# One VectorE product for two states at a time in a selective scan that runs beside attention

## The chip, the cores and the metric

One Trainium2 chip, one core of it. The metric is the device time of one execution in microseconds (us). The kernel before took a median of 3411.59 us in 3 runs (3409.64 to 3413.27).

## The reference, cut to what matters

The input is a batch of 4 images, 128 channels of 64 x 64. Four layers follow one another: attention over the 4096 positions with a residual (layer 0), two quantized 3 x 3 convolutions (layer 1), a Mamba block with a group norm (layer 2), and attention again (layer 3). The change is in layer 2. Its core is a scan over the 4096 positions of an image, for 256 inner channels and 16 states each:

```python
def step(h, inp):
    dt_t, B_t, C_t, x_t = inp
    dA = jnp.exp(dt_t[..., None] * A)
    dBx = dt_t[..., None] * B_t[:, None, :] * x_t[..., None]
    h = dA * h + dBx
    y = jnp.einsum('bdn,bn->bd', h, C_t)
    return (h, y)
...
return jnp.swapaxes(ys, 0, 1) + xc * D
```

`B_t` and `C_t` are the same for all channels and differ by state; `A` differs by channel and state.

## The kernel before, in words

**Tiling.** The 256 inner channels lie as 128 partitions x 2 halves (index h). The 4096 positions of an image are cut into 8 blocks of 512 (TB). A *group* g is one block of one image: 4 images x 8 blocks are 32 groups, and each has 16 states n. One *state* m = 16 g + n is the unit of the scan: 512 of them. Tiles that hold both halves of one block are 128 x 2 x 512 fp32, 1024 elements in a partition.

**What one state does.** Nine instructions, the load among them:

- fetch (SP's queue, L1086): row n of B and row n of C, repeated over all 128 partitions, into a `bc` tile (3 buffers); it may start when the product with C of three states earlier is done;
- decays (ScalarE, L1099, one for each half): `da = exp(A dt)` into PSUM, one buffer for each half, so it waits for the scan that read the last one;
- the **B product** (VectorE, L1126): `hs = ud * B`, with `ud = dt x`, 1024 elements, for both halves in one instruction; `hs` has 3 buffers, so it waits for the addition of three states earlier;
- the **scans** (VectorE, L1134, one for each half, 512 elements): `hs[t] = da[t] hs[t-1] + hs[t]` in place, which begins from `hlast`, the last column of the block before;
- the last column (ScalarE, L1109): copied from `hs` to `hlast` before `hs` is overwritten, except in an image's last block;
- the **C product** (VectorE, L1116): `hs = hs * C` in place, which waits for that copy;
- the **addition** (GpSimd, L1151): `y = y + hs`, which waits for the C product.

After the 16th state of a group GpSimd also does the **gate** (L1155), `y = y * sz`. VectorE's order is B product of state m, C product of state m - 1, the two scans of state m.

**Preparation of a group** (L884 to L996). TensorE, ScalarE and VectorE make `xc`, `sz`, `dt`, `ud` and the start of `y` from layer 1's output. The softplus for `dt` uses a tile `sp` (Abs at L971, Exp at L976, read last by VectorE at L982), followed by L984, L986 and L990 on VectorE.

**Everything else runs beside it.** While layer 2 works on one image, TensorE and ScalarE do an attention stage of another. The eight attention stages follow each other in the order layer 0 of images 0, 1 and 2, layer 3 of 0, layer 0 of 3, layer 3 of 1, 2 and 3. The last has no scan beside it. An attention stage makes blocks of energies (L535), their exponentials (ScalarE, L553) and the products with the values (L615, L624, L643). Layer 0's operands are split into a high and a low part by way of a tile `h` (L443 and L445). The convolutions' instructions on VectorE are L804, L816, L833, L838 and L840; those at the end of an attention block are L694, L705, L735 and L765; L1020 and L1062 belong to the group norm.

**What sets the order.** All instructions are written by chains (generators: `scans`, `additions`, `fetches`, `preparation`, `convolutions`, `energies` and so on). Before each instruction a chain yields an `op`: engine, planned time, the marks that it needs, and flags. The class `Order` keeps a clock for every engine and always takes the chain whose next instruction has the lowest key, planned start + 0.15 x the chain's rank on that engine (`RANKS`). The outcome is a fixed order of each engine's queue; on the chip an instruction waits only for the data and buffers that it needs. One flag matters here: `port=True` for VectorE instructions, and always for GpSimd, books a planner's clock that both share, so that the plan never lays two such instructions over each other. On the chip nothing enforces this part of the plan.

Of the kernel before, what the change touches and what calls it, by code (L numbers as in the profile page):

```python
# [8 lines left out]
F32 = mybir.dt.float32  # L9
# [11 lines left out]
P = 128  # L21
# [10 lines left out]
DS = 16  # L32
# [17 lines left out]


RANKS = {
    "layer1_weights": dict(SP=-5.3, ACT=9.6, DVE=17.6, PE=-7.5),
    "layer2_weights": dict(SP=11.2, ACT=5.6, DVE=13.0),
    "parts": dict(ACT=0.8),
    "first": dict(ACT=-1.6, DVE=-2.8, PE=-4.9),
    "convolutions": dict(ACT=2.0, DVE=4.4, PE=4.2),
    "preparation": dict(SP=16.0, PE=2.4, ACT=0.9, DVE=3.0),
    "output": dict(PE=3.0, ACT=0.0, DVE=1.7, SP=-3.8),
    "lasts": dict(ACT=-0.0),  # L60
    "energies": dict(PE=3.5),
    "exponentials": dict(ACT=1.4),
    "products": dict(PE=5.1),
    "decays": dict(ACT=0.8),
    "scans": dict(DVE=4.7),
    "additions": dict(POOL=9.6),
    "fetches": dict(SP=-17.0),
    "accumulations": dict(DVE=15.7),
    "totals": dict(PE=-1.0),
    "images": dict(SP=9.9),  # L70
    "high_low": dict(ACT=4.8, DVE=2.3),
    "copy": dict(ACT=2.5),
    "finish0": dict(DVE=2.9, ACT=-1.9, PE=-5.1),
    "stage_input": dict(SP=9.0),
    "residual": dict(SP=2.8),
    "finish3": dict(PE=4.1, DVE=3.8, ACT=3.2, SP=-14.6),
}


class Order:  # L80
# [7 lines left out]
    def __init__(self):  # L88
        self.clock = dict(PE=7.0, ACT=5.0, DVE=6.0, POOL=6.0, SP=7.0)
        self.marks = {}  # L90
        self.chains = []
        self.table = self.tiles = None
        self.bank = 0.0
        self.port = 0.0
        self.end = (0.0, None)

# [9 lines left out]
    def mark(self, *key):  # L106
        self.marks[key] = self.end
# [1 line left out]
    def known(self, time, *key):  # L109
        self.marks[key] = time, None  # L110

    def release(self):
        self.bank = self.end[0]

    def run(self):
        while self.chains:
            best = None
            for item in self.chains:
                engine, time, needs, bank, table, port, lag, tiles, who = item[3]
                if any(k not in self.marks for k in needs) or (bank and self.bank is None):  # L120
                    continue
                start = self.clock[engine]
                for t, e in [item[2], *(self.marks[k] for k in needs)]:
                    start = max(start, t + (self.HOP if e != engine else 0.0))
                if bank:
                    start = max(start, self.bank + self.HOP)
# [12 lines left out]
            item[2] = self.clock[engine], engine  # L139
            self.end = self.clock[engine] + lag, engine  # L140
            if bank:
                self.bank = None
# [35 lines left out]
def conv_seq_kernel(ctx: ExitStack, tc: tile.TileContext, i: dict, out: bass.AP):  # L178
# [107 lines left out]
    def layer1_weights(k):  # L286
        unit, dt = ((LEVELS, F32R), (LEVELS * LEVELS, FP8))[k - 1]
        yield op("SP", 0.3, lag=4.0)
        w = mam.tile([P, 2, TB], F32, tag="hs", name=f"w{k}", bufs=3)
# [127 lines left out]
    def operands(s):  # L417
# [19 lines left out]
        def high_low(o, g, key, bias, low, n):  # L437

            c = len(lows)
            lows.append(("low", s, c))  # L440
            yield op("ACT", 0.2 + n * 1e-3, (*key, "in"), *lows[c - 1 : c])
            h = att.tile([P, 2 * TB], F32R, tag="h", name="h", bufs=1)
            nc.scalar.activation(h[:, 0:n], g, AF.Identity, bias=low[1], scale=low[0])  # L443
            yield op("DVE", 0.06 + n * 1.2e-3)
            nc.vector.scalar_tensor_tensor(o, g, bias, h[:, 0:n], ALU.add, ALU.subtract)  # L445
            mark(*key)
            mark(*lows[c])

# [113 lines left out]
    def accumulations():  # L562
        for t in filter(added, range(len(stages) * NS)):
            k, q = divmod(t, NQ)
            for h in range(2):
# [4 lines left out]
                    need.append(("total", k - 1))  # L570
                yield op("DVE", 1.25, *need, port=True)
                if q == 0:
                    accs[k] = att.tile([P, 2, 2, CB], F32, tag="acc", name="acc", bufs=1)
                other = ps[t, 0] if q == 0 else accs[k]
                nc.vector.tensor_add(accs[k], ps[t, h], other)  # L575
            mark("acc", t)
# [307 lines left out]
    def preparation():  # L884
        for g in range(NG + 1):
# [70 lines left out]
            for h in range(2):  # L956
                yield op("PE", 0.98, *need, bank=True, who=who)
                if h == 0:
                    dt, ud, y = (pair(t, t, 2) for t in ("dt", "ud", "y"))
                    a = pair("sp", "sp", 1)  # L960
                ps = gtile("dt_ps")
                for k in range(2):
                    nc.tensor.matmul(
# [3 lines left out]
                        start=True,  # L967
                        stop=True,
                    )
                yield op("ACT", 0.69, who=who)  # L970
                nc.scalar.activation(a[:, h, :], ps, AF.Abs, bias=bdt[:, h : h + 1])  # L971
                yield op("ACT", 0.68, who=who)
                nc.scalar.activation(dt[:, h, :], ps, AF.Relu, bias=bdt[:, h : h + 1])
                release()
            yield op("ACT", 1.06, table="exp", who=who)
            nc.scalar.activation(a, a, AF.Exp, scale=-1.0)  # L976
# [3 lines left out]
            nc.scalar.activation(ud, y, AF.Ln)  # L980
            yield op("DVE", 1.22, port=True, who=who)
            nc.vector.scalar_tensor_tensor(y, y, 1.0, a, ALU.subtract, ALU.subtract)  # L982
            yield op("DVE", 1.22, port=True, who=who)
            nc.vector.tensor_sub(ud, ud, y)  # L984
            yield op("DVE", 1.22, port=True, who=who)
# [92 lines left out]
                mark("x2", b, k)  # L1078

    def fetches():  # L1080
        for m in range(NM):
            g, n = divmod(m, DS)
            need = [("c", m - 3)] if m > 2 else []
            yield op("SP", 0.1, ("bc_d", g), *need, lag=5.0)
            bcs[m] = bc = mam.tile([P, 2, TB], F32, tag="bc", name="bc", bufs=3)
            nc.sync.dma_start(  # L1086
                out=bc, in_=live["bc", g][:, n, :].unsqueeze(0).to_broadcast([P, 2, TB])
            )
            if n == DS - 1:
                live.pop(("bc", g))  # L1090
            mark("bc", m)

    def decays(h):
        for m in range(NM):
# [7 lines left out]
            mark("da", m, h)  # L1102

    def lasts():
        for m in range(NM):
            g, n = divmod(m, DS)
            if g % NTB < NTB - 1:
                yield op("ACT", 0.2, ("s", m, 1))
                nc.scalar.copy(hlast[:, n, :], hss[m][:, :, TB - 1])  # L1109
                mark("last", m)  # L1110
            else:
                order.known(0.0, "last", m)

    def readout(m):
        hs = hss[m]
        nc.vector.tensor_mul(hs, hs, bcs.pop(m)[:, 1:2, :].to_broadcast([P, 2, TB]))  # L1116
        mark("c", m)

    def scans():
        for m in range(NM):  # L1120
            g, n = divmod(m, DS)
            need = [("add", m - 3)] if m > 2 else []
            yield op("DVE", 1.2, ("bc", m), ("ud", g), *need, port=True)
            ud = live["in", g][1]
            hss[m] = hs = pair("hs", "hs", 3)
            nc.vector.tensor_mul(hs, ud, bcs[m][:, 0:1, :].to_broadcast([P, 2, TB]))  # L1126
            if n == 0:
                mark("begun", g)
            if m:
                yield op("DVE", 1.13, ("last", m - 1), port=True)  # L1130
                readout(m - 1)
            for h in range(2):
                yield op("DVE", 1.19, ("da", m, h))
                nc.vector.tensor_tensor_scan(  # L1134
                    hs[:, h, :],
                    das.pop((m, h)),
                    hs[:, h, :],
                    hlast[:, n, h : h + 1] if g % NTB else 0.0,
                    ALU.mult,
                    ALU.add,  # L1140
                )
                mark("s", m, h)
        yield op("DVE", 1.13, ("last", NM - 1), port=True)
        readout(NM - 1)

    def additions():
        for m in range(NM):
            g, n = divmod(m, DS)
            yield op("POOL", 2.36, ("c", m), ("y", g))
            y = live["in", g][2]  # L1150
            nc.gpsimd.tensor_tensor(y, y, hss.pop(m), ALU.add)  # L1151
            mark("add", m)
            if n == DS - 1:
                yield op("POOL", 2.4, ("sz", g))
# [534 lines left out]
```

## Time and profile before

| what | value |
|---|---|
| median of the runs | 3411.59 us |
| the profiled execution, its own time | 3404.14 us |
| its span (first to last instruction) | 3402.3 us |
| busy TensorE, VectorE, ScalarE, GpSimd | 3123.7, 3024.0, 2573.9, 1319.4 us |
| mean granted TensorE clock | 0.979 |
| additions L1151 / gates L1155 on GpSimd | 512 of 2376 ns / 32 of 3127 ns |
| decays L1099 on ScalarE | 1024 of 690 ns |
| fetches L1086, 512 KB each, issue to landing | 512, median 4.8 us (3.4 to 9.0) |
| first and last scan | 173 us and 3076 us |

How it is read: in a line of instruction groups come the line and engine, the operation, output and inputs with shape and type, the count, then busy time and mean ns of one, then the engine's idle time just before these instructions and what ended most of it. In a list of waits come the waiting engine, tile and line, what ended the wait, the total us, how many times, and the longest. In a timeline come start and length in us, engine, line, operation, the tiles, the count, and in brackets the idle time before it. VectorE's instructions overlap in it by some 0.08 us, so costs are read from start to start. GpSimd's lengths include any time in which an issued instruction stood still.

### The profile page before, as it was taken

How to read it: one execution, taken by the hardware profiler on the slowest of the kernel's cores; microseconds unless marked ns; L12 is line 12 of the kernel's file. 1: busy time of each engine (PE TensorE's matmuls, PEld its weight loads, DVE VectorE, ACT ScalarE, POOL GpSimd, SP SyncE). 2: the span in 40 equal slices, each digit the busy share in tenths (PEclk: the TensorE clock that was granted, in tenths of full speed). 3: DMA queues.
4: the chain of work that ended last, by engine and by line, in shares of the span. 5: the costliest groups of instructions: out<-in, count | busy, mean ns of one | idle time of the engine just before them, and what ended most of it. 6: DMA issues, size and time to landing. Idle time of an engine off the chain costs nothing.

```text
span 3402.3 us, 69611 instructions
## 1 busy us (share of the span) xinstructions
PE 3123.7 (92%) x29359; PEld 2249.8 (66%) x29359; DVE 3024.0 (89%) x2828; ACT 2573.9 (76%) x3899; POOL 1319.4 (39%) x565
## 2 busy tenths in 40 slices
PE   7999989999889999998988999999899899998998
PEld 5887768788678776555547888755455455555665
DVE  3199999999999999999999999999999999994554
ACT  4588877878788786878777888877788787865554
POOL 0044444444334444444434444444444445441000
PEclk9999999999999999999999999999999999999999
DMA  3033343333443334444443333444444444330000
GB/s 80 23 97 101 89 121 97 98 101 98 111 111 101 97 94 125 105 110 109 111 138 97 97 91 93 120 97 110 124 111 108 130 104 116 105 111 18 8 11 12
DMA packets 194179, 321.72 MB, mean 95 GB/s; under 512 B 44352, under 2 KB 46784, under 8 KB 193856
## 3 DMA queue, kind: packets, MB, share of 16 engines
q1 hardware_dynamic: 193568, 316.32, 35.1%
q8 instruction: 232, 3.80, 0.4%
q10 hardware_dynamic: 288, 0.85, 0.1%
q14 instruction: 91, 0.75, 0.1%
HBM read 300.35 MB, written 16.78 MB: 93 GB/s over the span
## 4 chain that ended last, share of the span: by engine, by line
DVE 50%; PE 29%; issue 10%; ACT 9%; DMA 2%; SPq 0%; DVEq 0%; ACTq 0%
DVE hs L1134 21%; DVE hs L1126 12%; DVE hs L1116 9%; PE e L535 8%; PE us L624 6%; PE us L615 6%; ACT p L553 2%; ACT da L1099 2%; PE us L643 1%; DMA bc<-bc_d 1%; DVE ud L984 1%; PE proj L458 1%; PE proj L500 1%; PE conv L777 1%; ACT L1099 1%
## 5 line engine op out<-in xcount | busy, mean ns | idle before, releaser
L1151 POOL TENSOR_TENSOR y<-y,hs 128x1024 f32<-128x1024 f32 x512 | 1216.7, 2376 | 1751.3 <-DVE hs L1116 1699.0
L553 ACT ACTIVATE p<-e 128x1024 f32<-128x1024 f32 x1024 | 1011.3, 1017 | 186.1 <-PE e L535 86.5
L1134 DVE TENSOR_TENSOR_SCAN hs<-da,hlast,hs 128x512 f32<-128x512 f32 x896 | 1098.8, 1263 | 8.2 <-ACT da L1099 8.1
L615 PE MATMUL us<-v,p 128*128 128x129 f32 x8192 | 1028.7, 281 | 16.4 <-ACT us L671 16.4
L615 PEld LDWEIGHTS us<-v,p 128*128 128x128 f32 x8192 | 959.6, 193 | 79.1 <-ACT us L671 22.7
L1099 ACT ACTIVATE da<-dt,late 128x512 f32<-128x512 f32 x1024 | 701.5, 690 | 249.8 <-DVE hs L1134 247.0
L1116 DVE TENSOR_TENSOR hs<-hs,bc 128x1024 f32<-128x1024 f32 x512 | 674.0, 1316 | 20.7 <-ACT hlast L1109 20.5
L1126 DVE TENSOR_TENSOR hs<-ud,bc 128x1024 f32<-128x1024 f32 x512 | 661.0, 1291 | 0.4
L535 PE MATMUL e<-it,v 64*128 64x256 f32 x4096 | 543.6, 401 | 64.3 <-ACT p L553 63.1
L624 PE MATMUL us<-p,v 128*32 128x256 f32 x8192 | 512.7, 386 | 22.0 <-ACT ss L680 22.0
L535 PEld LDWEIGHTS e<-it,v 64*128 64x128 f32 x4096 | 374.9, 190 | 222.6 <-ACT p L553 115.5
L624 PEld LDWEIGHTS us<-p,v 128*32 128x32 f32 x8192 | 244.8, 110 | 243.6 <-issue 70.3
L535 PE MATMUL e<-it,j 64*128 64x256 f32 x2048 | 222.4, 319 | 42.4 <-ACT p L553 39.2
L535 PEld LDWEIGHTS e<-it,j 64*128 64x128 f32 x2048 | 146.1, 187 | 127.3 <-ACT p L553 67.4
L643 PE MATMUL us<-p,ones 128*32 128x256 f32 x3072 | 204.3, 383 | 0.0
L575 DVE TENSOR_TENSOR acc<-p,acc 128x1024 f32<-128x1024 f32 x96 | 117.4, 1223 | 60.4 <-ACT p L553 56.1
L1109 ACT COPY hlast<-hs 128x2 f32<-128x2 f32 x448 | 84.8, 189 | 102.3 <-DVE hs L1134 93.5
L1134 DVE TENSOR_TENSOR_SCAN hs<-da,hs 128x512 f32<-128x512 f32 x128 | 149.4, 1203 | 0.9 <-ACT da L1099 0.8
L643 PEld LDWEIGHTS us<-p,ones 128*32 128x32 f32 x3072 | 89.5, 110 | 81.2 <-issue 32.6
L875 PEld LDWEIGHTS <-w 128*128 128x128 bf16 x576 | 53.4, 99 | 88.0 <-issue 47.3
L875 PE MATMUL xh<-x,w 128*128 128x512 fp8e4 x384 | 93.6, 380 | 8.5 <-ACT sz L898 5.8
L1155 POOL TENSOR_TENSOR y<-y,sz 128x1024 f32<-128x1024 f32 x32 | 100.1, 3127 | 2.5
(173 smaller groups left out, 2532.3 us busy)
## 6 DMA issues: line engine op xcount, KB each, us to landing
bc<-bc_d SPq DMA_DIRECT2D x512, 512.0 KB, 4.8
x_in<-in_x SPq DMA_DIRECT2D x16, 512.0 KB, 7.5
xpad<-in_x SPq DMA_DIRECT2D x32, 256.0 KB, 4.2
x_d<-yo SPq DMA_DIRECT2D x24, 256.0 KB, 2.9
x_in<-x_d SPq DMA_DIRECT2D x12, 512.0 KB, 7.3
o<-x_d SPq DMA_DIRECT2D x24, 256.0 KB, 5.3
out<-o SPq DMA_DIRECT2D x24, 256.0 KB, 2.5
bc_d<-xd SPq DMA_DIRECT2D x64, 32.0 KB, 4.2
```

The costliest lines, as they stand in the source:

```text
L535: nc.tensor.matmul(e[h][:, k % 2, k // 4, :], lhsT=jts[s][row : row + D3, col : col + P], rhs=its[s][row : row + D3, c * CB : (c + 1) * CB ...
L553: nc.scalar.activation(p, es[t][h], AF.Exp)
L575: nc.vector.tensor_add(accs[k], ps[t, h], other)
L615: nc.tensor.matmul(us[:, r, 0:VP], lhsT=ps[t, h][:, k % 2, k // 4, r * P : (r + 1) * P], rhs=vts[s][:, 8 * q + k, :], start=q == 0 and k = ...
L624: nc.tensor.matmul(us[m : m + 32, 0, :], lhsT=vts[s][:, 8 * q + k, m % D3 : m % D3 + 32], rhs=ps[t, h][:, k % 2, k // 4, :], start=q == 0 ...
L643: nc.tensor.matmul(us[32 * m : 32 * m + 32, 1, :], lhsT=ones[:, 0:32], rhs=term, start=False, stop=q == NQ - 1 and k >= len(terms) - 4,)
L875: nc.tensor.matmul(g, lhsT=w3[:, k // len(rhs), lhs[k % len(rhs)] : lhs[k % len(rhs)] + P], rhs=x[:, rhs[k % len(rhs)]], start=(k == 0), s ...
L1099: nc.scalar.activation(da, live["in", g][0][:, h, :], AF.Exp, scale=amat[:, h, n : n + 1])
L1116: nc.vector.tensor_mul(hs, hs, bcs.pop(m)[:, 1:2, :].to_broadcast([P, 2, TB]))
L1126: nc.vector.tensor_mul(hs, ud, bcs[m][:, 0:1, :].to_broadcast([P, 2, TB]))
L1134: nc.vector.tensor_tensor_scan(hs[:, h, :], das.pop((m, h)), hs[:, h, :], hlast[:, n, h : h + 1] if g % NTB else 0.0, ALU.mult, ALU.add,)
L1151: nc.gpsimd.tensor_tensor(y, y, hss.pop(m), ALU.add)
```

## The change

- The B product is made for two states in one instruction of 2048 elements, and so is the C product. `hs` becomes 128 x 2 states x 2 halves x 512, still with 3 buffers.
- VectorE's order becomes: B product of states 2k and 2k + 1, scans of state 2k, C product of states 2k - 2 and 2k - 1, scans of state 2k + 1. One product stands between two pairs of scans, where there were two.
- B and C rows come in separate fetches, each for two states; each of the two tiles has one buffer, so a fetch waits for the product that read the last one. Their number (512) and size stay.
- The last columns of two states are copied at once.
- The additions stay one for each state, 1024 elements; two of them wait for the same C product.
- `sp` moves into the buffer of the `h` tile, with a lock in the planner between preparation and layer 0's operand split, and `acc` (the last stage's sum) moves into the buffer of `xc`. Relu now comes before Abs.
- The planned times of products and scans and nearly all ranks are new. The `w` tile of the weights is adapted to the new `hs` shape.

```diff
 RANKS = {
-    "layer1_weights": dict(SP=-5.3, ACT=9.6, DVE=17.6, PE=-7.5),
-    "layer2_weights": dict(SP=11.2, ACT=5.6, DVE=13.0),
...
-    "convolutions": dict(ACT=2.0, DVE=4.4, PE=4.2),
-    "preparation": dict(SP=16.0, PE=2.4, ACT=0.9, DVE=3.0),
...
-    "scans": dict(DVE=4.7),
-    "additions": dict(POOL=9.6),
-    "fetches": dict(SP=-17.0),
...
+    "layer1_weights": dict(SP=16.9, ACT=7.3, DVE=19.5, PE=10.0),
+    "layer2_weights": dict(SP=-20, ACT=-12.9, DVE=8.4),
...
+    "convolutions": dict(ACT=3.1, DVE=2.4, PE=3.4),
+    "preparation": dict(SP=20, PE=2.3, ACT=0.9, DVE=1.0),
...
+    "scans": dict(DVE=3.8),
+    "additions": dict(POOL=8.5),
+    "fetches": dict(SP=20),
...
-            yield op("ACT", 0.2 + n * 1e-3, (*key, "in"), *lows[c - 1 : c])
+            yield op("ACT", 0.2 + n * 1e-3, (*key, "in"), *lows[c - 1 : c], bank="h")
...
+            release("h")
...
-                    accs[k] = att.tile([P, 2, 2, CB], F32, tag="acc", name="acc", bufs=1)
+                    accs[k] = mam.tile([P, 2, 2, CB], F32, tag="xc", name="acc", bufs=1)
...
-                    a = pair("sp", "sp", 1)
...
-                yield op("ACT", 0.69, who=who)
-                nc.scalar.activation(a[:, h, :], ps, AF.Abs, bias=bdt[:, h : h + 1])
                 yield op("ACT", 0.68, who=who)
                 nc.scalar.activation(dt[:, h, :], ps, AF.Relu, bias=bdt[:, h : h + 1])
+                yield op("ACT", 0.69, who=who, bank=False if h else "h")
+                if h == 0:
+                    a = att.tile([P, 2, TB], F32, tag="h", name="sp", bufs=1)
+                nc.scalar.activation(a[:, h, :], ps, AF.Abs, bias=bdt[:, h : h + 1])
...
     def fetches():
-        for m in range(NM):
-            g, n = divmod(m, DS)
-            need = [("c", m - 3)] if m > 2 else []
+        for k, which in [(0, 0)] + [
+            (k + 1 - w, w) for k in range(NM // 2) for w in (0, 1) if k + 1 - w < NM // 2
+        ]:
+            g, n = divmod(2 * k, DS)
+            tag = "bc"[which]
+            need = [(tag, k - 1)] if k else []
             yield op("SP", 0.1, ("bc_d", g), *need, lag=5.0)
-            bcs[m] = bc = mam.tile([P, 2, TB], F32, tag="bc", name="bc", bufs=3)
+            bcs[tag, k] = t = pair(f"{tag}_n", f"{tag}_n", 1)
             nc.sync.dma_start(
-                out=bc, in_=live["bc", g][:, n, :].unsqueeze(0).to_broadcast([P, 2, TB])
+                out=t,
+                in_=live["bc", g][which, n : n + 2, :].unsqueeze(0).to_broadcast([P, 2, TB]),
             )
...
     def lasts():
-        for m in range(NM):
-            g, n = divmod(m, DS)
+        for k in range(NM // 2):
+            g, n = divmod(2 * k, DS)
             if g % NTB < NTB - 1:
-                yield op("ACT", 0.2, ("s", m, 1))
-                nc.scalar.copy(hlast[:, n, :], hss[m][:, :, TB - 1])
-                mark("last", m)
+                yield op("ACT", 0.2, ("s", 2 * k + 1, 1))
+                nc.scalar.copy(hlast[:, n : n + 2, :], hss[k][:, :, :, TB - 1])
+                mark("last", k)
...
     def scans():
         for m in range(NM):
             g, n = divmod(m, DS)
-            need = [("add", m - 3)] if m > 2 else []
-            yield op("DVE", 1.2, ("bc", m), ("ud", g), *need, port=True)
-            ud = live["in", g][1]
-            hss[m] = hs = pair("hs", "hs", 3)
-            nc.vector.tensor_mul(hs, ud, bcs[m][:, 0:1, :].to_broadcast([P, 2, TB]))
-            if n == 0:
-                mark("begun", g)
-            if m:
-                yield op("DVE", 1.13, ("last", m - 1), port=True)
-                readout(m - 1)
-            for h in range(2):
-                yield op("DVE", 1.19, ("da", m, h))
+            k = m // 2
+            if m % 2 == 0:
+                need = [("add", m - 5)] if m > 4 else []
+                yield op("DVE", 2.22, ("b_n", k), ("ud", g), *need, port=True)
+                hss[k] = hs = mam.tile([P, 2, 2, TB], F32, tag="hs", name="hs", bufs=3)
+                nc.vector.tensor_mul(
+                    hs,
+                    live["in", g][1].unsqueeze(1).to_broadcast([P, 2, 2, TB]),
+                    bcs.pop(("b", k)).unsqueeze(2).to_broadcast([P, 2, 2, TB]),
+                )
+                mark("b", k)
+                if n == 0:
+                    mark("begun", g)
+            elif k:
+                yield op("DVE", 2.19, ("last", k - 1), ("c_n", k - 1), port=True)
+                readout(k - 1, 0, 2)
+                mark("c", k - 1)
+            for h in range(2):
+                yield op("DVE", 1.13 if g % NTB == 0 else 1.19, ("da", m, h))
                 nc.vector.tensor_tensor_scan(
-                    hs[:, h, :],
+                    hs[:, m % 2, h, :],
                     das.pop((m, h)),
-                    hs[:, h, :],
+                    hs[:, m % 2, h, :],
                     hlast[:, n, h : h + 1] if g % NTB else 0.0,
...
     def additions():
         for m in range(NM):
             g, n = divmod(m, DS)
-            yield op("POOL", 2.36, ("c", m), ("y", g))
+            yield op("POOL", 2.36, ("c", m // 2), ("y", g))
             y = live["in", g][2]
-            nc.gpsimd.tensor_tensor(y, y, hss.pop(m), ALU.add)
+            hs = hss[m // 2] if m % 2 == 0 else hss.pop(m // 2)
+            nc.gpsimd.tensor_tensor(y, y, hs[:, m % 2], ALU.add)
             mark("add", m)
```

More of the change, by code (lines that the diff above doesn't have):

```diff
@@ L52 @@
 RANKS = {
-    "layer1_weights": dict(SP=-5.3, ACT=9.6, DVE=17.6, PE=-7.5),
-    "layer2_weights": dict(SP=11.2, ACT=5.6, DVE=13.0),
-    "parts": dict(ACT=0.8),
-    "first": dict(ACT=-1.6, DVE=-2.8, PE=-4.9),
-    "convolutions": dict(ACT=2.0, DVE=4.4, PE=4.2),
-    "preparation": dict(SP=16.0, PE=2.4, ACT=0.9, DVE=3.0),
[L59 to L63, printed above, removed]
-    "decays": dict(ACT=0.8),
-    "scans": dict(DVE=4.7),
-    "additions": dict(POOL=9.6),
-    "fetches": dict(SP=-17.0),
[L68 to L76, printed above, removed]
+    "layer1_weights": dict(SP=16.9, ACT=7.3, DVE=19.5, PE=10.0),
+    "layer2_weights": dict(SP=-20, ACT=-12.9, DVE=8.4),
+    "parts": dict(ACT=0.4),
+    "first": dict(ACT=-5.6, DVE=-5.9, PE=1.7),
+    "convolutions": dict(ACT=3.1, DVE=2.4, PE=3.4),
+    "preparation": dict(SP=20, PE=2.3, ACT=0.9, DVE=1.0),
+    "output": dict(PE=3.2, ACT=2.1, DVE=-3.4, SP=3.7),
+    "lasts": dict(ACT=1.4),
+    "energies": dict(PE=3.3),
+    "exponentials": dict(ACT=1.9),
+    "products": dict(PE=5.0),
+    "decays": dict(ACT=0.8),
+    "scans": dict(DVE=3.8),
+    "additions": dict(POOL=8.5),
+    "fetches": dict(SP=20),
+    "accumulations": dict(DVE=15.1),
+    "totals": dict(PE=-4.2),
+    "images": dict(SP=-1.0),
+    "high_low": dict(ACT=0.4, DVE=0.5),
+    "copy": dict(ACT=2.8),
+    "finish0": dict(DVE=1.2, ACT=-19.6, PE=-5.5),
+    "stage_input": dict(SP=20),
+    "residual": dict(SP=2.1),
+    "finish3": dict(PE=4.7, DVE=4.3, ACT=3.8, SP=10.5),
 }
@@ L92, in __init__ @@
         self.table = self.tiles = None
-        self.bank = 0.0
+        self.locks = {True: 0.0, "h": 0.0}
         self.port = 0.0
@@ L110, in known, with release @@
         self.marks[key] = time, None
-    def release(self):
-        self.bank = self.end[0]
+    def release(self, lock=True):
+        self.locks[lock] = self.end[0]
     def run(self):
@@ L119, in run @@
                 engine, time, needs, bank, table, port, lag, tiles, who = item[3]
-                if any(k not in self.marks for k in needs) or (bank and self.bank is None):
+                if any(k not in self.marks for k in needs) or (bank and self.locks[bank] is None):
                     continue
@@ L125, in run @@
                 if bank:
-                    start = max(start, self.bank + self.HOP)
+                    start = max(start, self.locks[bank] + self.HOP)
                 if port:
@@ L141, in run @@
             if bank:
-                self.bank = None
+                self.locks[bank] = None
             if port:
@@ L288, in layer1_weights @@
         yield op("SP", 0.3, lag=4.0)
-        w = mam.tile([P, 2, TB], F32, tag="hs", name=f"w{k}", bufs=3)
+        w = mam.tile([P, 2, 2, TB], F32, tag="hs", name=f"w{k}", bufs=3)[:, 0]
         last = att.tile([P, TB], F32, tag="t", name=f"w{k}_8", bufs=1)[:, 0:P]
@@ L982, in preparation @@
             nc.vector.scalar_tensor_tensor(y, y, 1.0, a, ALU.subtract, ALU.subtract)
+            release("h")
             yield op("DVE", 1.22, port=True, who=who)
@@ L1080, in fetches @@
     def fetches():
-        for m in range(NM):
-            g, n = divmod(m, DS)
-            need = [("c", m - 3)] if m > 2 else []
+        for k, which in [(0, 0)] + [
[4 more added lines that the diff above has]
+            need = [(tag, k - 1)] if k else []
             yield op("SP", 0.1, ("bc_d", g), *need, lag=5.0)
-            bcs[m] = bc = mam.tile([P, 2, TB], F32, tag="bc", name="bc", bufs=3)
+            bcs[tag, k] = t = pair(f"{tag}_n", f"{tag}_n", 1)
             nc.sync.dma_start(
-                out=bc, in_=live["bc", g][:, n, :].unsqueeze(0).to_broadcast([P, 2, TB])
+                out=t,
+                in_=live["bc", g][which, n : n + 2, :].unsqueeze(0).to_broadcast([P, 2, TB]),
             )
-            if n == DS - 1:
+            if which and n == DS - 2:
                 live.pop(("bc", g))
-            mark("bc", m)
+            mark(f"{tag}_n", k)
     def decays(h):
@@ L1104, in lasts @@
     def lasts():
-        for m in range(NM):
-            g, n = divmod(m, DS)
+        for k in range(NM // 2):
+            g, n = divmod(2 * k, DS)
             if g % NTB < NTB - 1:
-                yield op("ACT", 0.2, ("s", m, 1))
-                nc.scalar.copy(hlast[:, n, :], hss[m][:, :, TB - 1])
-                mark("last", m)
-            else:
[L1112 to L1117, printed above, removed]
+                yield op("ACT", 0.2, ("s", 2 * k + 1, 1))
+                nc.scalar.copy(hlast[:, n : n + 2, :], hss[k][:, :, :, TB - 1])
+                mark("last", k)
+            else:
+                order.known(0.0, "last", k)
     def scans():
@@ L1142, in scans, with readout @@
                 mark("s", m, h)
-        yield op("DVE", 1.13, ("last", NM - 1), port=True)
-        readout(NM - 1)
+        yield op("DVE", 2.19, ("last", k), ("c_n", k), port=True)
+        readout(k, 0, 2)
+        mark("c", k)
+    def readout(k, a, b):
+        hs = hss[k][:, a:b]
+        nc.vector.tensor_mul(
+            hs, hs, bcs.pop(("c", k))[:, a:b].unsqueeze(2).to_broadcast([P, b - a, 2, TB])
+        )
     def additions():
```

## The prediction

> **What bounds the kernel now.** I read the page first (busy shares, costliest groups), then the waits, then the busy time by stretches, then the timelines of VectorE and GpSimd. The page gives the two engines that are nearly full and the four groups of lines that the change touches:
>
> ```profile
> PE 3123.7 (92%) x29359; PEld 2249.8 (66%) x29359; DVE 3024.0 (89%) x2828; ACT 2573.9 (76%) x3899; POOL 1319.4 (39%) x565
> ...
> L1151 POOL TENSOR_TENSOR y<-y,hs 128x1024 f32<-128x1024 f32 x512 | 1216.7, 2376 | 1751.3 <-DVE hs L1116 1699.0
> ...
> L1134 DVE TENSOR_TENSOR_SCAN hs<-da,hlast,hs 128x512 f32<-128x512 f32 x896 | 1098.8, 1263 | 8.2 <-ACT da L1099 8.1
> ...
> L1116 DVE TENSOR_TENSOR hs<-hs,bc 128x1024 f32<-128x1024 f32 x512 | 674.0, 1316 | 20.7 <-ACT hlast L1109 20.5
> L1126 DVE TENSOR_TENSOR hs<-ud,bc 128x1024 f32<-128x1024 f32 x512 | 661.0, 1291 | 0.4
> ```
>
> The 89% is an average with an idle head and tail. Inside the scan stage (first scan 173 us, last 3076) VectorE has no holes to speak of:
>
> ```profile
> 2800.00:3000.00 200.00, 186.03 (x2178) 108.78 (x2180) 196.14 (x168) 158.85 (x250) 94.72 (x39) 0.97 0.39 108
> ```
>
> The columns after the length are PE, PEld, DVE, ACT and POOL: VectorE 196 of 200 us, TensorE 186. Scans and the two products wait for nearly nothing (0.4, 8.2 and 20.7 us); everybody else waits for them:
>
> ```profile
> POOL y L1151 <- DVE hs L1116: 1699.0, 492, 174.9
> ACT da L1099 <- DVE hs L1134: 247.0, 261, 3.9
> ...
> DVE hs L1116 <- ACT hlast L1109: 20.5, 18, 4.5
> ```
>
> So the end is set by VectorE's chain until 3077 us, then by a last attention stage of some 300 us on TensorE that the change leaves alone. What one state costs is seen in a quiet stretch of VectorE (start, length):
>
> ```profile
> 1523.26 1.30 DVE L1126 TENSOR_TENSOR hs<-ud,bc 128x1024 f32<-128x1024 f32 x1
> 1524.48 1.21 DVE L1116 TENSOR_TENSOR hs<-hs,bc 128x1024 f32<-128x1024 f32 x1
> 1525.62 2.45 DVE L1134 TENSOR_TENSOR_SCAN hs<-da,hlast,hs 128x512 f32<-128x512 f32 x2
> 1527.98 1.30 DVE L1126 TENSOR_TENSOR hs<-ud,bc 128x1024 f32<-128x1024 f32 x1
> ```
>
> From start to start: B product 1.22, C product 1.14, two scans 2.36, a state 4.72. And GpSimd beside it:
>
> ```profile
> 1525.84 2.36 POOL L1151 TENSOR_TENSOR y<-y,hs 128x1024 f32<-128x1024 f32 x1 [2.36 <-DVE hs L1116]
> ```
>
> The addition starts 0.22 after the C product's end and runs exactly under the two scans, then GpSimd idles 2.36 us under the two products. That fit matters more for this change than the lengths of the products.
>
> **Part 1, merged products.** 512 B products and 512 C products of 1024 elements become 256 and 256 of 2048. The C product advances 1.13 to 1.14 for 1024 elements; L1020 (one input, 512 elements) advances 0.61, so (1.13 - 0.61)/512 is 1.02 ns an element and 2048 give 2.17. The durations of plain adds (L575 1223 ns at 1024, L765 678 at 512) give 1.06 ns and 2.23. I take 2.20: 0.07 saved per merge. A B product advances 1.12 where no addition runs into it (1504.43 to 1505.55) and 1.22 where the addition's last 0.22 us overlaps it; two such waits of 0.09 become one. A pair of states: 9.44 before; 2 x 2.36 + 2.20 + 2.29 = 9.21 after. 0.23 x 256 = **59 us off**. Ends: merges alone, 512 x 0.07 = 36; 2.17 for both and no wait, 0.38 x 256 = 97.
>
> The trace gives 1223 ns for an fp32 sum of two SBUF tensors of 1024. [...]
>
> **Part 2, one copy of last columns for two states.** 448 copies of 189 ns become 224: 42 us off ScalarE, which is not the bound. The C product's wait for it (20.5 us in 18 waits) goes: between odd scans and that product now lie a B product and two scans, 4.6 us, more than the longest wait of 4.5. **20 us off**, ends 0 and 20.5.
>
> **Part 3, two additions at a time.** Now a C product frees two additions at once. The first runs under the odd state's scans as before. The second is ready at once behind it, and GpSimd's queue holds nothing that makes it wait for the next pair of scans. The trace shows what two GpSimd operations back to back do, since each group of 16 states ends with addition and gate (L1155). VectorE:
>
> ```profile
> 1199.11 2.44 DVE L1134 TENSOR_TENSOR_SCAN hs<-da,hlast,hs 128x512 f32<-128x512 f32 x2
> 1201.48 1.30 DVE L1126 TENSOR_TENSOR hs<-ud,bc 128x1024 f32<-128x1024 f32 x1
> 1202.70 3.37 DVE L1116 TENSOR_TENSOR hs<-hs,bc 128x1024 f32<-128x1024 f32 x1
> ```
>
> and GpSimd:
>
> ```profile
> 1199.33 2.37 POOL L1151 TENSOR_TENSOR y<-y,hs 128x1024 f32<-128x1024 f32 x1 [2.36 <-DVE hs L1116]
> 1201.78 3.22 POOL L1155 TENSOR_TENSOR y<-y,sz 128x1024 f32<-128x1024 f32 x1
> ```
>
> The two engines take turns. The B product was there when the addition ended and went first; the gate waited 0.85 us, ran from the B product's end, and the C product behind stood still: 3.37 instead of 1.21. If VectorE is late, GpSimd goes first:
>
> ```profile
> 1111.58 3.10 DVE L1126 TENSOR_TENSOR hs<-ud,bc 128x1024 f32<-128x1024 f32 x1
> ```
>
> Here a L705 between the scans let the gate start at 1111.23, and the B product took 3.10. Scans never suffer.
>
> The row first: VectorE lost 2.16 or 1.89 us and no half speed was seen. [...]
>
> In a quiet pair the new order survives: B product first, second addition from its end under the even scans, C product free. [...] From the timeline, 235 to 3078 us, counting groups of other VectorE instructions over 0.25 us by what they follow: 118 after two scans, 42 after a C product, 38 after a B product, 25 between scans. Half of 118 (59), 30 of the 42 (the rest are single two-input ones, which only delay the addition), 12 of the 25 and 16 of the 38 do harm: 117, which spread at random hit 256 x (1 - e^(-117/256)) = 94 pairs. The other end is the gates themselves: of 32, four held a B product (636, 726, 1111, 2021 us), which gives 32 of 256. I take the middle, 63, at (2.16 + 1.89)/2 = 2.03: **128 us on**, ends 65 and 191. The gates' own 32 collisions stay as they are.
>
> **Part 4, what I cost at nothing.** Fetches: 512 of 512 KB before and after; the single B buffer leaves 9.21 - 2.29 = 6.9 us from product to product, three buffers left 2 x 4.72 - 2.36 = 7.1, and nothing waited then (landing 4.8 median, 9.0 at most). Cover gone: 28 x_in loads on SP's queue each delaying one fetch by 9.0 - 6.9, 59 us. SP has as many issues as before, in another order. *sp* in *h*: held some 20 us (L971 2952 to L982 2972), so three attention starts could each wait that long, behind TensorE's slack; cover gone 60. Relu and Abs swap; acc takes *xc* after its last use: nothing. Ranks: head and tail within 10 us either way, the size of the head's longest single load wait (cwb, 10.1).
>
> **Sum.** The profiled execution took 3404.14 (span 3402.3, 1.8 around it): 3404.1 - 59 - 20 + 128 = 3453. The median of the runs is 7.4 above the profiled one: **3460**.
>
> **Rivals.** *B, faster.* The slips stay rare, because the new ranks put other work in the even half, where GpSimd has finished. Decides below (59 + 20)/2.03 = 39 slips. At 16, 3404 - 79 + 32 + 7 = 3365; at none 3332, with the best merge 3294. For it: gates slipped only 4 times in 32. Against: the plan's clock books products and additions as exclusive but lets the plan choose who goes first, and the chip chose GpSimd whenever it waited. TensorE allows it: from 200 to 3080 us it is busy 2647 of 2880; at the tail's 193 of 202 it would need 2774, a floor 106 us down.
>
> *C, no change.* The attention stream is as late as the scans: its last products before the tail end at 3092, the last Silu at 3099. If it cannot close up, VectorE's gain turns into idle time: 3404 + 7 = 3411.
>
> *D, it does not do what it says*: a product that repeats both operands runs slower than one element a step. The B product already repeats one at 1.12; I give it nothing of its own.
>
> **Chances.** Forecast (slips outweigh) 0.55, 3419 to 3546 (191 on, 36 and 20 off, 7). B 0.36, C 0.09. A measurement tells 0.2% (6.8 us). The range 3340 to 3530 drops the last tenth of B and of the forecast.
>
> **What would show it.** Right: B and C products near 2.2 to 2.3 where quiet; some 60 products, or instructions next to them, over 4 us or 2 us too long, beside the second of two additions; GpSimd's idle time before additions in long stretches, not one per state; hlast copies 224 and no wait for them. Wrong: fewer than 39 long ones; waits of a B product for its fetch; VectorE under 95% busy in the scan stage, which would put the bound on TensorE or ScalarE.

## The result, and the profile after

The changed kernel takes 3533.57 us (median of 4 runs, 3528.63 to 3534.68) against 3412.43: 1.0353 of the time before, 95% interval 1.0335 to 1.0371. The direction was forecast, the size was not: +121 us instead of +48, just outside the range, which ended at 3530. The profiled execution took 3533.13 us, its span is 3531.3. The page's first part and the four groups (the additions are now L1168, scans L1143, B products L1129, C products L1158):

```profile
PE 3176.9 (90%) x29359; PEld 2275.8 (64%) x29359; DVE 3139.5 (89%) x2316; ACT 2554.6 (72%) x3673; POOL 1623.4 (46%) x565
...
L1168 POOL TENSOR_TENSOR y<-y,hs 128x1024 f32<-128x1024 f32 x512 | 1532.1, 2992 | 1581.4 <-DVE hs L1158 1519.1
...
L1143 DVE TENSOR_TENSOR_SCAN hs<-da,hlast,hs 128x512 f32<-128x512 f32 x896 | 1102.4, 1268 | 27.8 <-ACT da L1106 7.7
...
L1129 DVE TENSOR_TENSOR hs<-ud,b_n 128x2048 f32<-128x2048 f32 x256 | 683.0, 2668 | 1.1 <-POOL y L1168 0.2
L1158 DVE TENSOR_TENSOR hs<-hs,c_n 128x2048 f32<-128x2048 f32 x256 | 613.2, 2395 | 4.2 <-ACT hlast L1116 3.4
```

VectorE issues 512 instructions fewer and is busy 115 us longer. The two groups of products together fell only from 1335 to 1296 us, and an addition went from 2376 to 2992 ns on average: both contain time in which an issued instruction stood still. A disturbed pair of states and a quiet one on VectorE:

```profile
1507.26 0.70 DVE L1023 BATCH_NORM_STATS2 stats<-yo 128x6 f32<-128x512 f32 x1
1507.87 2.44 DVE L1143 TENSOR_TENSOR_SCAN hs<-da,hlast,hs 128x512 f32<-128x512 f32 x2
1510.23 4.16 DVE L1129 TENSOR_TENSOR hs<-ud,b_n 128x2048 f32<-128x2048 f32 x1
...
1533.27 2.39 DVE L1129 TENSOR_TENSOR hs<-ud,b_n 128x2048 f32<-128x2048 f32 x1
1535.76 2.46 DVE L1143 TENSOR_TENSOR_SCAN hs<-da,hlast,hs 128x512 f32<-128x512 f32 x2
1538.14 2.26 DVE L1158 TENSOR_TENSOR hs<-hs,c_n 128x2048 f32<-128x2048 f32 x1
```

and GpSimd's additions beside them, two to a line (length of both together):

```profile
1507.41 4.83 POOL L1168 TENSOR_TENSOR y<-y,hs 128x1024 f32<-128x1024 f32 x2 [2.67 <-DVE hs L1158]
...
1531.13 6.76 POOL L1168 TENSOR_TENSOR y<-y,hs 128x1024 f32<-128x1024 f32 x2 [7.04 <-DVE hs L1158]
```

In the quiet pair the two additions span 6.76 us: 2.36 under the odd scans, 2.0 of standing still behind the B product, 2.36 under the even scans. In the disturbed pair a 0.6 us L1023 delayed the odd scans; both additions ran through in 4.83, and the B product stood still for 1.9. All 46 B products that were held up in this way have another instruction in the odd half.

The second thing to see is the quiet B product. From its start to the scan's it is 2.49 us here (median of the run 2.46; C products of the same size 2.18), and behind its end there is a gap of 0.10 where elsewhere instructions overlap by 0.08. Some 0.10 of the 2.46 is the overlap with the end of an addition, as before; without additions it is 2.37.

**Where the time went.** I summed VectorE's timeline of the scan stage from start to start, idle time apart. "Too long" are instructions more than 0.4 us above the 20th percentile of their group; their time is inside the other columns, and a product in two halves counts as one. The rows without additions, "changed, B product in two" and the last one are single executions; executions of one kernel lie up to 13 us apart here (the kernel before: 3405.70 to 3418.12). All in us.

| kernel | median | B products | C products | scans | others | idle | too long (count) |
|---|---|---|---|---|---|---|---|
| before | 3412 | 624 | 634 | 1205 | 375 | 67 | 84 (42) |
| changed | 3534 | 703 | 590 | 1209 | 473 | 55 | 233 (124) |
| before, no additions | 3328 | 590 | 597 | 1206 | 346 | 88 | 30 (18) |
| changed, no additions | 3317 | 602 | 565 | 1210 | 344 | 88 | 16 (10) |
| the same, B product in two | 3292 | 585 | 565 | 1208 | 344 | 84 | 20 (12) |
| changed, held, new plan | 3469 | 652 | 566 | 1208 | 392 | 149 | 88 (46) |
| changed, held, same plan | 3422 | 659 | 568 | 1209 | 406 | 72 | 109 (61) |
| the same, B product in two | 3417 | 639 | 583 | 1207 | 406 | 78 | about 110 (64) |
| changed, B product in two | 3806 | 1021 | 558 | 1207 | 458 | 52 | about 560 (260) |
| one addition at a time | 3563 | 591 | 638 | 1209 | 383 | 238 | 90 (49) |
| the same, old ranks | 3467 | 584 | 643 | 1208 | 379 | 159 | 80 (44) |
| changed, old ranks | 3632 | 710 | 599 | 1207 | 464 | 122 | 240 (127) |
| before, new ranks | 3565 | 634 | 629 | 1205 | 408 | 190 | 107 (60) |
| the same, old rank of `lasts` | 3476 | 628 | 624 | 1207 | 377 | 140 | 79 (40) |

The stage runs from 173 to 3076 us before and from 180 to 3204 after: 7 us more ahead of it, 121 in it, and the tail behind it is the same (326 and 327). Of the 121, instructions held up are 149. They are 77 more on B products, 21 less on C products (which the gates used to hit) and 92 more on others: preparation (L984, L987), convolutions (L805, L817, L834 to L841) and norm (L1065).

### The profile page after: what moved, and what is told of

Same layout as the page of the kernel before. It is cut to its first block, busy times and chain, and to the rows that moved or that the text cites. A ratio compares the mean times of both kernels' runs of the same rounds, so it can differ in the third digit from the quotient of the medians.

```text
span 3531.3 us, 68609 instructions
## 1 busy us (share of the span) xinstructions
PE 3176.9 (90%) x29359; PEld 2275.8 (64%) x29359; DVE 3139.5 (89%) x2316; ACT 2554.6 (72%) x3673; POOL 1623.4 (46%) x565
## 2 busy tenths in 40 slices
DMA packets 128635, 321.65 MB, mean 91 GB/s; under 512 B 44352, under 2 KB 46784, under 8 KB 128320
## 5 line engine op out<-in xcount | busy, mean ns | idle before, releaser
L1168 POOL TENSOR_TENSOR y<-y,hs 128x1024 f32<-128x1024 f32 x512 | 1532.1, 2992 | 1581.4 <-DVE hs L1158 1519.1
L1143 DVE TENSOR_TENSOR_SCAN hs<-da,hlast,hs 128x512 f32<-128x512 f32 x896 | 1102.4, 1268 | 27.8 <-ACT da L1106 7.7
L616 PE MATMUL us<-v,p 128*128 128x129 f32 x8192 | 1046.6, 284 | 17.9 <-ACT us L672 17.8
L616 PEld LDWEIGHTS us<-v,p 128*128 128x128 f32 x8192 | 978.1, 196 | 80.2 <-ACT us L672 24.0
L1129 DVE TENSOR_TENSOR hs<-ud,b_n 128x2048 f32<-128x2048 f32 x256 | 683.0, 2668 | 1.1 <-POOL y L1168 0.2
L1158 DVE TENSOR_TENSOR hs<-hs,c_n 128x2048 f32<-128x2048 f32 x256 | 613.2, 2395 | 4.2 <-ACT hlast L1116 3.4
L536 PE MATMUL e<-it,j 64*128 64x256 f32 x2048 | 229.6, 323 | 96.1 <-ACT p L554 91.8
L1143 DVE TENSOR_TENSOR_SCAN hs<-da,hs 128x512 f32<-128x512 f32 x128 | 149.4, 1206 | 3.2 <-ACT p L554 0.5
L984 DVE SCALAR_TENSOR_TENSOR y<-y,sp 128x1024 f32<-128x1024 f32 x32 | 54.0, 1689 | 43.5 <-ACT ud L982 43.4
L1172 POOL TENSOR_TENSOR y<-y,sz 128x1024 f32<-128x1024 f32 x32 | 88.5, 2766 | 2.5
```

What stands on the lines that cost most here:

```text
L536: nc.tensor.matmul(e[h][:, k % 2, k // 4, :], lhsT=jts[s][row : row + D3, col : col + P], rhs=its[s][row : row + D3, c * CB : (c + 1) * CB ...
L616: nc.tensor.matmul(us[:, r, 0:VP], lhsT=ps[t, h][:, k % 2, k // 4, r * P : (r + 1) * P], rhs=vts[s][:, 8 * q + k, :], start=q == 0 and k = ...
L1129: nc.vector.tensor_mul(hs, live["in", g][1].unsqueeze(1).to_broadcast([P, 2, 2, TB]), bcs.pop(("b", k)).unsqueeze(2).to_broadcast([P, 2, 2 ...
L1143: nc.vector.tensor_tensor_scan(hs[:, m % 2, h, :], das.pop((m, h)), hs[:, m % 2, h, :], hlast[:, n, h : h + 1] if g % NTB else 0.0, ALU.mu ...
L1158: nc.vector.tensor_mul(hs, hs, bcs.pop(("c", k))[:, a:b].unsqueeze(2).to_broadcast([P, b - a, 2, TB]))
L1168: nc.gpsimd.tensor_tensor(y, y, hs[:, m % 2], ALU.add)
```

## The experiments

Theory L (in the expectations: lock and dependency): the second of two additions, always ready, takes turns with VectorE's products; and a scan right behind the B product that it reads waits for that product's end. Rival R: the new plan (ranks, the shared `h`) is worse, and the additions do not matter.

**Without additions, both kernels.** The edit in the changed kernel; in the kernel before, the addition becomes a bare `hss.pop(m)`.

```diff
-            nc.gpsimd.tensor_tensor(y, y, hs[:, m % 2], ALU.add)
```

> The changed kernel without its 512 additions on GpSimd (y keeps only its first term; the gates stay; every other queue in the same order). Theory L (lock and dependency): the changed kernel lost its time where the second of two additions held up VectorE (125 instructions too long, 234 us in all), so without additions no long instruction is left but a few beside gates, and a B product takes 2.36 from start to start instead of 2.46: 3533 - 234 - 26 = 3273, or a little above if TensorE then sets the end (its floor is about 3300): 3270 to 3320. Rival R (plan): the new ranks and the shared buffer h made a worse order; additions do not matter and the time stays above 3450.

> The kernel before without its 512 additions, same order of every other queue. Theory L: it loses its 42 long instructions (84 us) and the short waits of B products for an addition's end (0.09 on some 340): 3404 - 84 - 30 = 3290, a little above if TensorE sets the end: 3290 to 3330. With its partner the difference between the two kernels goes from +121 to within 30 of zero. Rival R: the difference between the two stays near +121.

Measured 3316.91 and 3328.06, one execution of each, both inside the forecast of theory L: +121 became -11. Theory L holds; of rival R only -11 is left to share between merging, last columns, ranks and buffers. Without additions the changed kernel needs 12 us more for its B products and 32 less for its C products.

**The B product in two instructions, without additions.**

```diff
-                nc.vector.tensor_mul(
-                    hs,
-                    live["in", g][1].unsqueeze(1).to_broadcast([P, 2, 2, TB]),
-                    bcs.pop(("b", k)).unsqueeze(2).to_broadcast([P, 2, 2, TB]),
-                )
+                bt = bcs.pop(("b", k))
+                for j in range(2):
+                    nc.vector.tensor_mul(
+                        hs[:, j], live["in", g][1], bt[:, j : j + 1, :].to_broadcast([P, 2, TB])
+                    )
```

> As the changed kernel without additions, but each B product for two states is issued as two instructions of 1024 elements, state by state, in the same place. Theory L: the scans that follow a B product wait for its full end, because they read what it has just written (0.18 from start to start); in two instructions the first scans read what the earlier one wrote and need not wait: 1.13 + 1.13 = 2.26 instead of 2.36, 0.10 x 256 = 26 us less on VectorE although there are 256 instructions more. Without such a wait two instructions cost 0.07 more each time, 18 us more.

Measured 3291.87, 25 us less with 256 instructions more, as theory L forecast (26); 17 of them stand in the column of the B products. VectorE without additions, in one instruction

```profile
1499.70 2.28 DVE L1129 TENSOR_TENSOR hs<-ud,b_n 128x2048 f32<-128x2048 f32 x1
1502.08 2.46 DVE L1143 TENSOR_TENSOR_SCAN hs<-da,hlast,hs 128x512 f32<-128x512 f32 x2
1504.45 2.26 DVE L1158 TENSOR_TENSOR hs<-hs,c_n 128x2048 f32<-128x2048 f32 x1
1506.64 2.45 DVE L1143 TENSOR_TENSOR_SCAN hs<-da,hlast,hs 128x512 f32<-128x512 f32 x2
```

and in two:

```profile
1499.05 2.33 DVE L1131 TENSOR_TENSOR hs<-ud,b_n 128x1024 f32<-128x1024 f32 x2
1501.30 2.44 DVE L1143 TENSOR_TENSOR_SCAN hs<-da,hlast,hs 128x512 f32<-128x512 f32 x2
```

Start to start: 2.38 for the merged B product, 2.19 for the equally long C product whose successor does not read it, 2.25 for the two halves. The stall (2.38 against 2.19) costs more than the merge saves (2.19 against 2.25).

**The second addition held back.** One more wait: an odd state's addition may start only when the next B product is done.

```diff
-            nc.gpsimd.tensor_tensor(y, y, hs[:, m % 2], ALU.add)
+            add = nc.gpsimd.tensor_tensor(y, y, hs[:, m % 2], ALU.add)
...
+                tc.add_manual_dep(
+                    add.ins,
+                    b_ins[m // 2 + 2].ins.name,
...
```

> The changed kernel with one more wait: the addition of each odd state waits until the next B product is done, so it cannot slip ahead of it. Theory L: the 46 long B products (86 us) go, and with them most long instructions ahead of B products (L839, L841, L984, L987, L805 and others between odd scans and B product, 115 us in all, of which about two thirds): 3533 - 86 - 75 = 3370 to 3450. Rival R: as before this edit, 3533 within 20, or more, since GpSimd is only made later.

Measured 3468.59 (1.017, 1.015 to 1.0189), a little above the forecast. The instructions held up fell as forecast (88 us), but the edit had also entered the planner, and in the new plan VectorE idled 149 us. So once more with every queue in its old order:

> The changed kernel with every queue in the same order, and one more wait only: the addition of an odd state waits for the end of the next B product (237 of 256 of them; in the other 19 the plan has them ahead of it). The earlier run with this wait had a new plan as well, in which VectorE's idle time in the scan stage rose from 55 to 149 us. Theory L: long instructions fall from 124 (233 us) to about 46 (88 us) as there, idle time stays near 55: 3533 - 145 = 3390, 3370 to 3420. If the idle time comes with the wait itself and not with the plan: again about 3470.

Measured 3421.64 (1.004, 1.0026 to 1.0054), 2 us above the forecast of theory L: some 110 of the 121 us are gone with one wait, on an engine that is busy for 46% of the changed kernel's span. The kernel is again as fast as the one before, not faster. VectorE and GpSimd now:

```profile
1504.36 2.45 DVE L1143 TENSOR_TENSOR_SCAN hs<-da,hlast,hs 128x512 f32<-128x512 f32 x2
1506.73 2.37 DVE L1129 TENSOR_TENSOR hs<-ud,b_n 128x2048 f32<-128x2048 f32 x1
1509.20 2.46 DVE L1143 TENSOR_TENSOR_SCAN hs<-da,hlast,hs 128x512 f32<-128x512 f32 x2
```

```profile
1504.58 2.36 POOL L1170 TENSOR_TENSOR y<-y,hs 128x1024 f32<-128x1024 f32 x1 [2.38 <-DVE hs L1158]
1509.24 2.37 POOL L1170 TENSOR_TENSOR y<-y,hs 128x1024 f32<-128x1024 f32 x1 [2.29 <-DVE hs L1129]
```

Each addition lies under a pair of scans again, released once by the C product and once by the B product. The idle time did come mostly with the plan (72 here, 149 there, 55 without the wait). Of the instructions too long, 61 are left, not 46; one kind is seen at 1516 us, where a gate pushed the next addition back and the B product behind it took 4.42.

> As the run with the same plan and the wait, and each B product in two instructions of 1024 elements, the wait being for the second. Theory L: without the stall before the scans another 25 us go, as they did without additions: 3350 to 3395, below its partner and perhaps below the kernel before. If a second addition still gets between the two halves it is far above its partner.

Measured 3416.59 (1.0016, 1.0007 to 1.0026): above the forecast and 5 us below its partner, not 25. B products fell by 20 us, and C products rose by 15: their start-to-start median went from 2.18 to 2.28. Instructions held up stayed the same. VectorE and GpSimd:

```profile
1508.92 2.44 DVE L1143 TENSOR_TENSOR_SCAN hs<-da,hlast,hs 128x512 f32<-128x512 f32 x2
1511.29 2.36 DVE L1158 TENSOR_TENSOR hs<-hs,c_n 128x2048 f32<-128x2048 f32 x1
```

```profile
1509.14 2.36 POOL L1170 TENSOR_TENSOR y<-y,hs 128x1024 f32<-128x1024 f32 x1 [2.36 <-DVE hs L1131]
```

Behind the two halves the addition starts 0.22 us after the scans, where it started 0.04 after them, so it ends 0.21 after the C product's start (0.04 with the B product in one). The stall had been covering that overlap.

**The B product in two, with nothing held.**

> The changed kernel with each B product in two instructions and no added wait. Theory L: the second addition stands ready when a B product begins and now gets its turn between the two halves; the second half is held up by some 2.1 us in the quiet pairs as well (about 170 of 256): 3533 + 170 x 2.1 - 25 = 3865, 3750 to 3950. Without the turn-taking: 3508, as the 25 us that the two halves saved without additions.

Measured 3805.74, one execution, inside the forecast of theory L. An edit worth -25 us without additions costs 272 with them. VectorE and GpSimd:

```profile
1606.25 2.44 DVE L1143 TENSOR_TENSOR_SCAN hs<-da,hlast,hs 128x512 f32<-128x512 f32 x2
1608.62 4.59 DVE L1131 TENSOR_TENSOR hs<-ud,b_n 128x1024 f32<-128x1024 f32 x2
1613.13 2.44 DVE L1143 TENSOR_TENSOR_SCAN hs<-da,hlast,hs 128x512 f32<-128x512 f32 x2
```

```profile
1606.47 5.65 POOL L1168 TENSOR_TENSOR y<-y,hs 128x1024 f32<-128x1024 f32 x2 [5.78 <-DVE hs L1158]
```

The two halves take 4.51 instead of 2.25: the addition that waited gets its turn between them and ends at 1612.12. So it goes in 158 of the 256 pairs, and in 39 more the first half is held up. In these runs the engine that waits is served when the other's instruction ends, even if the other's next instruction is already queued, so a product waits for more than the data and buffers that it needs.

**One addition at a time.** B products stay merged; each state has its own C product, C row and copy again, two states behind the scans.

```diff
-            elif k:
-                yield op("DVE", 2.19, ("last", k - 1), ("c_n", k - 1), port=True)
-                readout(k - 1, 0, 2)
-                mark("c", k - 1)
+            if m > 1:
+                yield op("DVE", 1.13, ("last", m - 2), ("c_n", m - 2), port=True)
+                readout(m - 2)
...
```

> The changed kernel with the C products undone: B products for two states stay, but each state has its own C product, C row (256 KB) and copy of last columns again, two states behind the scans, so that every pair of scans follows a C product and one addition at a time becomes ready. Theory L: the second addition never stands ready, long instructions fall back to about those of the kernel before (84 us), and no B product stands right before a scan that reads it. A pair of states: 2.20 + 2 x 1.14 + 4.72 + 2 x 0.09 = 9.38 against 9.44 before, -15 us, and no wait for last columns, -17: 3375 to 3410. Rival R: the new ranks and the shared h remain, so it stays near 3533, at least above 3480.

> The same kernel with the ranks of before. Theory L: 3375 to 3420, within 20 of its partner. Rival R: about 100 below its partner.

Measured 3562.85 (1.0448, 1.043 to 1.0465) and 3466.53 (1.0166, 1.0149 to 1.0183). Both times, and the 96 us between them, are what rival R forecast, and theory L was wrong on them by some 150 and 50 us. What theory L said of the instructions held up came true: they fall to 90 and 80 us, and B products to 591 and 584. But VectorE idles 238 and 159 us: it waits for ScalarE in preparation (L984, 69 and 73 us) and for decays (36 and 56). The old ranks take off 79 us of the idle time. The order is new throughout, and whether the rest belongs to the structure or to ranks that were not made for it, these runs do not tell.

**The ranks, crosswise.**

> The kernel before with only the new ranks. Theory L: 3412 within 20. Rival R: 3500 or more, most of the +121.

> The changed kernel with the ranks of before. Theory L: 3500 to 3560, since what collides is set by the products' order. Rival R: back near 3412 to 3440.

Measured 3565.35 (1.0458, 1.0441 to 1.0476) and 3632.05 (1.0653, 1.0636 to 1.0671). Theory L missed the first (3412 within 20), and rival R had it (3500 or more): the new ranks alone cost the old kernel 155 us. Both missed the second. The new ranks did not bring the changed kernel's loss: with the old ranks it is 98 us slower still, instructions held up are the same 240 us, and idle time is 122 instead of 55. What the new ranks do to the kernel before:

```profile
DVE hs L1116 <- ACT hlast L1109: 106.4, 115, 8.0
```

That wait was 20.5 us before and is 3.4 in the changed kernel. The old order has one product of 1.2 us between scans and C product, the new one 4.6 us. Restoring this one rank:

> The kernel before with the new ranks except that of the copies of last columns (ScalarE rank 0.0 as before, not 1.4). With the new ranks its C products waited 106 us for those copies (20.5 before), most of its 155 us. Theory: that rank is what the old order of products could not stand, and the changed order can (3.4 us of such waits): 3430 to 3500. If the ranks as a whole make a worse order: above 3540.

Measured 3475.53, one execution: 90 of the 155 us, inside the forecast. Ranks fit one order of products, and a swap across kernels measures the misfit.

## Why the prediction was wrong, point by point

- **The bound** was right: VectorE's stage grew by 121 us, the tail stayed, and without additions the stage fell to 2804 us, so TensorE left room (there it is busy 2642 of the 2800 us from 200 to 3000).
- **Part 1, merged products: the step that failed.** I took 59 us; apart from instructions held up, B products rose by 2 and C products fell by 23: 21 us. A quiet pair costs 2 x 2.36 + 2.46 + 2.18 = 9.36, not 9.21: the B product takes 2.46 where the sum has 2.29 (44 us over 256 pairs), the C product 2.18 where it has 2.20. I gave the B product the advance of an instruction whose successor does not read it. The row was in the trace of before: the very first B product, followed by its scan, advances 1.33 (172.07 to 173.40), and L986 and L990, each read by the one behind, 1.26, against 1.13. The sum had to include the wait of a consumer that the change moves next to its producer on one engine.

```profile
169.55 1.22 DVE L986 TENSOR_TENSOR dt<-dt,ud 128x1024 f32<-128x1024 f32 x1
170.81 1.23 DVE L990 TENSOR_TENSOR ud<-dt,xc 128x1024 f32<-128x1024 f32 x1
172.07 1.23 DVE L1126 TENSOR_TENSOR hs<-ud,bc 128x1024 f32<-128x1024 f32 x1
173.40 2.34 DVE L1134 TENSOR_TENSOR_SCAN hs<-da,hs 128x512 f32<-128x512 f32 x2
```

- **Part 2** was right in size: the wait fell from 20.5 to 3.4 us; idle time as a whole fell by 12.
- **Part 3, slips: right mechanism, size too small.** I took 63 at 2.03, 128 us; measured 82 more held up, at 1.81, 149 us. My own count of other work in the odd half (94) was the nearer end. That count has 12 of the 42 as single two-input instructions that only delay the addition, and 22 of the 38 as harmless; both were estimates of mine, and no run shows that the number of inputs decides. In the changed kernel L839 and L841, with one input, were held up 15 and 10 times in 32 (at most 2.48 us, median 0.43), and L1023, with one input too, never (0.67 to 0.70 us), though 26 of its 32 ran beside an instruction of GpSimd. The gates were a poor sample: in the timeline no preparation instruction lies between a gate's C product and its B product, while L984 and L987 alone are 18 of the 124.
- **Part 4** held. No B product waited for a fetch, `sp` in `h` left no mark of its own that I could separate (VectorE's wait for ScalarE ahead of preparation's L984 rose from 29.5 to 43.4 us, and no run tells why), the head grew by 7, inside the 10.
- In the sum, 38 us of gain too much in part 1, 21 of loss too little in part 3, 8 in part 2, 7 of head and some 10 of longer scans and others make 84. The table's columns add up to 4 us more than the stage grew, which leaves the 80 by which 3453 missed 3533. The forecast's own case reached 3546; the range was drawn narrower.
- **Rivals.** B needed fewer than 39 slips. C and D fell: everything followed VectorE, and without additions the B products, which repeat both operands, took 2.26 to 2.28 us each, C products of the same size 2.26. The turning point was also wrong: with 21 us of merging and 12 of waits it lies at (21 + 12)/1.81 = 18 slips.

## What to carry to other kernels

Here VectorE's products and GpSimd's additions took turns, and they fitted with little loss (0.10 us a state in the kernel before) while each addition was released just where VectorE had scans to do, none of which was held up (the 896 that read `hlast` took 1.25 to 1.29 us each); a merge that released two additions at once destroyed the fit (+121 us) though a pair of states got cheaper by 0.08 us, and one added wait on GpSimd restored some 110 us of it. Cost a merged instruction by its advance in front of its new neighbour: here a successor that reads its result does not overlap its end, which takes 0.18 us (2.36 against 2.18). And keep the order fixed when testing one mechanism, since a greedy planner turns an edit into a new plan: here that alone cost 47 us for the one added wait, and ranks made for another order cost 98 and 155.

## What the runs showed of the hardware that I had not expected

- **A dependent neighbour costs 0.18 us.** Without additions, B products of 2048 advance 2.36 to 2.38 in front of scans that read them, C products 2.18 to 2.19 in front of scans that do not: for a scan behind the product that it reads, the wait shows.
- **Fetches land sooner.** Two rows of one kind make one piece of 4 KB in each partition where there were two of 2 KB; packets fell from 194179 to 128635 for the same 512 fetches of 512 KB, and the median from 4.8 to 3.7 us. The x_in loads, whose shape did not change, land sooner too (7.5 to 6.3 us), so how much the longer pieces bring by themselves is not shown. No product had waited for a fetch before, so nothing in this kernel could use it.

```profile
b_n<-bc_d SPq DMA_DIRECT2D x256, 512.0 KB, 3.7
c_n<-bc_d SPq DMA_DIRECT2D x256, 512.0 KB, 3.7
```
